# Thirteen block products of a 1x1 convolution by quarter blocks, with other products' matmuls between them

## The chip, the cores and the metric

The kernel runs on one core of a Trainium2 chip. The metric is the device time of one execution in microseconds; before the change it is 2220.28 us, the median of three runs (2220.21 to 2221.42).

## What is computed

The reference is a residual block on 8 images of 512 channels and 32x32 pixels, all in fp32:

```python
t = cbs(gn(x), cv1_w, cv1_bn, 0)             # 1x1 conv 512 -> 512, batch norm, silu
ys = [t[:, :C], t[:, C:]]                    # C = 256
for i in range(N):                           # N = 2
    yi = ys[-1]
    z = cbs(yi, m_cv1_w[i], m_cv1_bn[i], 1)  # 3x3 conv 256 -> 256
    z = bot_attention(z, m_qkv_w[i], m_rw[i], m_rh[i])   # 4 heads, 1024 positions
    z = silu(bn_eval(conv2d(z, m_cv2_w[i], 0), m_cv2_bn[i]))
    ys.append(yi + z)
return x + cbs(concatenate(ys), cv2_w, cv2_bn, 0)        # 1x1 conv 1024 -> 512
```

The change concerns the last convolution, cv2, alone.

## The kernel before

The eight images are worked off in four passes of two images, ia and ib. TensorE (PE) does nearly all the work: cv1, the 3x3 convolutions in a Winograd form (matmuls c_ps<-v_in,u, with the weights u loaded from DRAM), the attention, m2, and cv2. A tile framework puts the instructions of each engine in an order at build time; each engine then works its queue off in order.

cv2 multiplies a weight matrix of 512 x 1024 by the 1024 channels of an image with 1024 pixels. Both are cut into 2 x 2 blocks (256 outputs by 512 channels; 512 channels by 512 pixels), and the product is done in the way of Strassen and Winograd with seven block products instead of eight. The left factors are the weight blocks "11", "12", "22" and their sums s1 to s4, which are made once and kept in DRAM (load_ws); the right factors are blocks of the concatenation, "top" (y0, y1) and "bottom" (y2, y3), and their sums t1 to t4. The products are M1 = 11 x top0, M2 = 12 x bottom0, M3 = s4 x bottom1, M5 = s1 x t1, M6 = s2 x t2, M7 = s3 x t3, M4 = 22 x t4. A block product (function product) is 8 matmuls: 4 chunks of 128 channels for each of two groups of 128 outputs, over 512 pixels.

In passes 0 to 2 strassen() does this for each image. M2 is accumulated in PSUM onto M1 (tile c_1, ps1), M3 onto M5 (c_5, ps5); part3 then does M6, M7, M4 one after the other, each in a new PSUM tile c_new, and VectorE (DVE) adds each to the kept m1 in one addition of 128x1024. Each finished block of 256 outputs by 512 pixels goes through finish(i): ScalarE (ACT) writes two tiles c_out (tag "t", four buffers, in turn), GpSimd's (POOL's) queue adds x to each by an accumulating DMA and stores them. For image ib the second conv stage of the next pass follows on PE right behind cv2, with its weights u in the same ring of ten SBUF tiles as the weight blocks. In that conv each of the steps takes two of three PSUM tiles of the pool ps_big; ACT copies one part out (c_m), DVE makes c_t and the rest.

In the last pass no work follows: rest_apart() has the products of both images apart, and m4_pieces() does the last product M4 of image ib in three pieces, of 512, 256 and 256 columns. finish_last() silus the pieces, DVE adds x from tiles x_res, and SP's queue stores them.

Of the kernel before, what the change touches and what calls it, by code (L numbers as in the profile page):

```python
# [61 lines left out]
def kernel(  # L62
# [237 lines left out]

    fed = {}

    def loader(key):
        kind = key[0]
        if kind == "u":
            _, n, oc, i, cp = key
            w = ring([P, NM, 2, 2, P], "u")
            nc.sync.dma_start(w, u_dram[n][oc][i][cp])
        elif kind == "sq":
            _, n, _, j = key  # L310
            at, size = SQ[j]
            w = ring([P, size, 3, P], "sq")
            nc.sync.dma_start(w, sq_dram[n][:, at : at + size])
        elif kind == "sw":
            at, size = SQ[key[2]]
            w = ring([P, size, NX // 2, C], "sw")
            nc.sync.dma_start(w, sw_dram[:, at : at + size])
        elif kind == "w1":
            w = ring([P, NX // 2, 2 * C], "w1")
            nc.sync.dma_start(w, cv1_w.rearrange("(k p) o -> p k o", p=P)[:, ts(key[2], NX // 2)])  # L320
        elif kind == "qkv":
            w = ring([P, 3 * C], "w_qkv")
            nc.sync.dma_start(w, m_qkv_w[key[1], ts(key[3], P), :])
        elif kind == "w2":
# [172 lines left out]
    def stages(act, small, ps_big, ps_av, n_pt):  # L497
# [45 lines left out]
        def tiles_steps(yp, put, is_=(0, 1, 2), ec=None, room=None, ec_at=("rs", 4)):  # L543
# [17 lines left out]
            for i in is_:  # L561
# [13 lines left out]
                nc.gpsimd.memset(e[:, :, 0:1], 0.0)  # L575
                cleared[0] = nc.gpsimd.memset(e[:, :, F + 1 : F + 2], 0.0)
# [767 lines left out]
        def strassen(b, ws, top, tags, tile_of):  # L1344
# [46 lines left out]
            def part3(bottom, after=None):  # L1391
                t1 = kept["t1"]
                t2, t3 = sums_tile("k"), tile_of("t3").rearrange("p a c (h w) -> p a c h w", w=F)
                with tc.issue_after(after.ins) if after else nullcontext():
                    for part in range(2):
                        tt(t2[:, part], bottom[1][part], t1[:, part], ALU.subtract)
                    for part in range(2):
                        tt(t3[:, part], bottom[1][part], top[1][part], ALU.subtract)
                t4 = sums_tile("q")
# [3 lines left out]
                w12, s4 = ws("12"), ws("s4")  # L1403
                for part in range(2):
                    product(ps1, w12, bottom[0], [part], onto=True)
                    product(ps5, s4, bottom[1], [part], onto=True)
# [16 lines left out]

            return part1, part1_more, part2, part3

        def sums_apart(top, bottom, t2, t3, t4):

            for part in range(2):
                tt(t3[part], bottom[1][part], top[1][part], ALU.subtract)
            for part in range(2):  # L1430
                last = tt(t2[part], t3[part], top[0][part], ALU.add)
            yield last
            for part in range(2):
                last = tt(t4[part], t2[part], bottom[0][part], ALU.subtract)
            yield last
# [29 lines left out]
        def rest_apart(ws, kept, bottom, t2, t3, t4, new, finish):  # L1465

            m1, m5 = kept["m1"], kept["m5"]
            pss, c12 = {}, []
# [23 lines left out]
            def m6():  # L1492
                tt(m1, raw("s2", t2), m1, ALU.add)
                tt(c12[0], c12[0], m1, ALU.add)
                finish(1, c12[0])

            def m7():
                tt(m1, raw("s3", t3), m1, ALU.add)
# [3 lines left out]
            def m4():  # L1502
                tt(m1, m1, raw("22", t4), ALU.subtract)
                finish(3, m1)

            def m4_pieces(out_of):
# [16 lines left out]
                m2_half=m2_half, m2_m3=m2_m3, add_m2=add_m2, add_m3=add_m3, m6=m6, m7=m7, m4=m4, m4_pieces=m4_pieces  # L1523
# [500 lines left out]
    for p in range(NP):  # L2024
# [365 lines left out]
        if p == 0:  # L2390
            ws = {name: load_ws(name) for name in ("21", "22", "11", "12")}
# [3 lines left out]
        else:  # L2395
            feed([("ws", p, name) for name in (WS_NAMES if more else ("12", "s4", "s2", "s3", "22"))])
# [7 lines left out]
        if more:  # L2404
            feed(units(0)[:3])
# [3 lines left out]
        def tile_of(name):  # L2409
            if not cz:  # L2410
                cz.append(act.tile([P, 4, 2 * HALF], F32, tag="z", name="cz"))
            if name == "t3":
                return cz[0][:, 0:2].rearrange("p a (c f) -> p a c f", c=NM)
            return cz[0][:, 3].rearrange("p (a f) -> p a f", a=2)

        bottom_a = [[side(Y2[0], half), img2(y3a[half])] for half in range(NH)]
        if not more:
# [14 lines left out]
            whole = [ring([P, HW], "x_res") for _ in range(NO)]  # L2432
            for oc in range(NO):
                nc.sync.dma_start(whole[oc], x[ib, ts(oc, P), :])
            ts_a = [], [], []
            rest_a = s.rest_apart(w_of, heads[ia].kept, bottom_a, *ts_a, acc_tile, s.finish_apart(ia))
# [7 lines left out]
            with tc.issue_after(end.evicted.ins):  # L2444
                last = next(sums_a)
            with tc.issue_after(last.ins):
                end.spread()
            with tc.issue_after(s.inverted[0].ins):
                rest_a.add_m2()
                last = next(sums_a)  # L2450
            with tc.issue_after(last.ins):
                scaled = end.scale()
            with tc.issue_after(scaled.ins):
                rest_a.add_m3()
            last = s.m2(1, z[:, :, 1], Y2[1], lambda oc, half: img(y3b[:, half, oc, :]))
            bottom = [[side(Y2[1], half), img2(y3b[:, half])] for half in range(NH)]
            top = load_tops(ib, Y1[1], "pt", 6)
            rest_a.m6()
# [7 lines left out]
            rest_b = s.rest_apart(w_of, heads[ib].kept, bottom, *ts_b, lambda: kept_sums.pop(0), finish)  # L2466
            rest_a.m7()
            rest_a.m4()
            for t, new in zip(ts_b, (wide("k"), pt_pair(), wide("q"))):
                t.extend(new)  # L2470
            for _ in s.sums_apart(top, bottom, *ts_b):
                pass
            rest_b.m2_half()
            rest_b.m2_m3()
            rest_b.add_m2()
            rest_b.add_m3()
            rest_b.m6()
            rest_b.m7()
# [22 lines left out]
        b1, b1_more, b2, b3 = s.strassen(ib, w_of, top, {"m1": ("p3", 1), "m5": ("p4", 1)}, tile_of)  # L2501
        b1()
        b1_more()
        b2()
        vs = v_units()
# [10 lines left out]
        for g in range(G):  # L2516
            s.tiles_in(Y1[g], putter(vs, g), [2], ecs[g])
# [109 lines left out]
```

## Time and profile before

| | |
|---|---|
| median of three runs | 2220.28 us |
| the profiled execution | 2222.78 us, of which the span of the profile 2221.2 us |
| PE busy | 2192.8 us, 99% of the span |
| DVE busy | 1752.2 us, 79% |
| ACT busy | 1093.9 us, 49% |
| POOL busy | 222.0 us, 10% |
| cv2 of image ib in pass 0, M5 to M4 | 593.20 to 634.50 us |
| last product, M4 of image ib in the last pass | starts at 2205.79 us |

Rows of a timeline give the start in us, the duration, the engine, the line of the kernel, the operation, output <- inputs, shape and how many instructions the row holds; in square brackets stands how long the engine had been idle before it, and what ended that. PEld is the loading of weights into PE, which runs beside its matmuls. A row with x16 spans sixteen instructions, from the start of the first to the end of the last. An fp32 matmul leaves two records. Rows of DMA issues give the time at which POOL or SP issued the transfer, not when it ended.

### The profile page before, as it was taken

The page shows a single profiled execution, that of the slowest core. Times are in us where ns is not written, and L with a number is a line of the kernel's source. Part 1 is how long each engine was busy: PE and PEld are TensorE (multiplying, and loading weights), DVE is VectorE, ACT ScalarE, POOL GpSimd, SP SyncE. Part 2 cuts the span into 40 slices and gives each one's busy share as a digit, 9 for nine tenths or more (in the row PEclk, how much of TensorE's full clock was granted, in tenths as well). Part 3 has the DMA queues.
Part 4 walks back from the last instruction along what each step waited for, and adds up shares of the span by engine and source line. Part 5 has one row for each costly group of instructions (what it writes and reads, how often), then busy time and mean ns, then how long its engine had stood idle before and what let it go on. Part 6 is the DMA issues. An engine that isn't in the chain of part 4 may idle for free.

```text
span 2221.2 us, 40357 instructions
## 1 busy us (share of the span) xinstructions
PE 2192.8 (99%) x16330; PEld 1079.8 (49%) x16330; DVE 1752.2 (79%) x2794; ACT 1093.9 (49%) x1320; POOL 222.0 (10%) x416
## 2 busy tenths in 40 slices
PE   7999999999999999999999999999999999999998
PEld 3653437343474444734447443654344734383433
DVE  8988879878769688977857868987785877897664
ACT  7454553554225666465323676455622465336543
POOL 4322210000220000000021000000002100000001
PEclk9999999999999999999999999999999999999999
DMA  8954447312582324512268141542126701261123
GB/s 265 317 170 136 168 149 260 105 64 68 142 264 68 119 82 132 199 59 68 63 162 267 31 166 36 190 131 77 58 67 171 268 30 44 91 208 34 58 59 96
DMA packets 133799, 285.61 MB, mean 129 GB/s; under 512 B 33541, under 2 KB 61185, under 8 KB 132581
## 3 DMA queue, kind: packets, MB, share of 16 engines
q1 hardware_dynamic: 101700, 197.34, 26.9%
q0 software_dynamic: 31904, 85.61, 13.2%
q8 instruction: 131, 2.15, 0.4%
q14 instruction: 64, 0.52, 0.1%
HBM read 214.86 MB, written 68.03 MB: 127 GB/s over the span
## 4 chain that ended last, share of the span: by engine, by line
PE 90%; DVE 6%; issue 1%; DMA 1%; ACT 1%; POOL 0%; DVEq 0%; ACTq 0%; POOLq 0%
PE av_ps L1101 19%; PE l_ps L1064 18%; PE c_ps L659 10%; PE c L1338 9%; PE c_new L1338 8%; PE p_ps L940 7%; PE m_ps L1318 5%; PE x_ps L1579 4%; PE ps L529 4%; PE p_ps L946 3%; PE s_ps L1119 1%; DMA taps<-in_m_cv_w_dram 1%; DVE acc L1085 1%; PE p_ps L904 1%; PE pv_ps L946 0%
## 5 line engine op out<-in xcount | busy, mean ns | idle before, releaser
L1068 ACT ACTIVATE pt<-l_ps 128x1024 f32<-128x1024 f32 x512 | 495.7, 1023 | 328.1 <-PE l_ps L1064 252.2
L1064 PE MATMUL l_ps<-q,kr 64*64 64x512 f32 x4096 | 485.5, 590 | 0.9 <-ACT pt L1068 0.9
L1101 PE MATMUL av_ps<-pt,vT 64*64 64x512 f32 x4096 | 484.7, 590 | 1.3 <-DVE z L1109 1.1
L1085 DVE TENSOR_TENSOR acc<-acc,pt 128x1024 f32<-128x1024 f32 x362 | 442.8, 1223 | 37.6 <-ACT pt L1068 11.2
L1101 PEld LDWEIGHTS av_ps<-pt,vT 64*64 64x64 f32 x4096 | 156.0, 133 | 280.7 <-issue 233.9
L1064 PEld LDWEIGHTS l_ps<-q,kr 64*64 64x64 f32 x4096 | 157.5, 133 | 270.3 <-issue 246.3
L659 PEld LDWEIGHTS c_ps<-v_in,u 128*64 128x64 f32 x4320 | 235.8, 137 | 6.3 <-issue 6.0
L659 PE MATMUL c_ps<-v_in,u 128*64 128x128 f32 x4320 | 238.5, 273 | 0.0
L1109 DVE TENSOR_TENSOR z<-av_ps,z 128x512 f32<-128x512 f32 x64 | 44.0, 688 | 98.4 <-ACT z L1108 98.3
L1318 PE MATMUL m_ps<-z,m_sb 128*128 128x512 f32 x256 | 113.9, 593 | 0.0
L664 ACT COPY c_m<-c_ps 128x512 f32<-128x512 f32 x48 | 28.1, 586 | 159.6 <-PE c_ps L659 145.9
L940 PE MATMUL p_ps<-t_z,sq 128*128 128x512 f32 x224 | 105.9, 595 | 0.0
L501 ACT ACTIVATE t<-m_ps,bh,sh 128x512 f32<-128x512 f32 x64 | 46.3, 774 | 94.0 <-PE m_ps L1318 92.8
L1082 DVE TENSOR_TENSOR acc<-pt 128x1024 f32<-128x1024 f32 x64 | 78.1, 1221 | 13.8 <-PE s_ps L1119 8.3
L940 PE MATMUL p_ps<-z,sq 128*128 128x512 f32 x168 | 81.3, 604 | 0.8 <-ACT z L501 0.7
L1318 PEld LDWEIGHTS m_ps<-z,m_sb 128*128 128x128 f32 x256 | 47.7, 190 | 56.7 <-issue 51.4
L1177 DVE TENSOR_TENSOR z<-z,rs 128x512 f32<-128x512 f32 x64 | 42.5, 687 | 26.9 <-DMA rs<-r_dram 26.7
L501 ACT ACTIVATE z<-z,bh,sh 128x512 f32<-128x512 f32 x64 | 48.7, 809 | 25.4 <-DVE z L721 25.2
L940 PEld LDWEIGHTS p_ps<-t_z,sq 128*128 128x128 f32 x224 | 39.5, 191 | 36.5 <-issue 34.4
L501 ACT ACTIVATE c_out<-m_kept,bh,sh 128x512 f32<-128x512 f32 (+1 forms) x33 | 38.9, 1276 | 34.6 <-issue 16.2
L1579 PE MATMUL x_ps<-t_x,sw 128*128 128x512 f32 x128 | 55.9, 592 | 0.0
L1338 PE MATMUL c_new<-t_in,wss 128*128 128x512 f32 x128 | 55.9, 592 | 0.0
(343 smaller groups left out, 3169.6 us busy)
## 6 DMA issues: line engine op xcount, KB each, us to landing
u<-u SPq DMA_DIRECT2D x135, 512.0 KB
y_in<-y SPq DMA_DIRECT2D x32, 512.0 KB
rs<-r_dram SPq DMA_DIRECT2D x126, 128.0 KB
sq<-sq SPq DMA_DIRECT2D x42, 384.0 KB
x<-in_x_dram SPq DMA_DIRECT2D x28, 512.0 KB
r_in<-r SPq DMA_DIRECT2D x28, 512.0 KB
c_out<-in_x_dram POOLq DMA_DIRECT2D x56, 256.0 KB, 5.5
out_dram<-c_out POOLq DMA_DIRECT2D x56, 256.0 KB, 3.3
```

The costliest lines, as they stand in the source:

```text
L501: silued[0] = nc.scalar.activation(dst, src, AF.Silu, scale=sh[:, k : k + 1], bias=bh[:, k : k + 1])
L529: last_product[0] = nc.tensor.matmul(ps[:, half, :], w_of(k), rhs_of(k, half), start=(k == begin), stop=(k == end))
L659: conv_product[0] = nc.tensor.matmul(to[o], us[cp][:, k, row, c, o], rhs, start=(k == 0), stop=(k == NM - 1),)
L940: nc.tensor.matmul(ps[:, o, :], w[:, o, :], rhs, start=not onto, stop=True, skip_group_check=onto)
L1064: nc.tensor.matmul(ps[kh * HD : (kh + 1) * HD, hd, :], kr[r, c, o : o + HD], q[r, c, ts(half, HALF)], start=True, stop=True,)
L1068: last_exp[0] = exp = nc.scalar.activation(pt, ps, AF.Exp, scale=SCALE)
L1082: return nc.vector.tensor_tensor(accs[g], pt[0], pt[1], ALU.add)
L1085: ins = nc.vector.tensor_tensor(accs[g], accs[g], pt[i], ALU.add)
L1101: nc.tensor.matmul(avs[g][hd * HD : (hd + 1) * HD, kh, :], vT[r, j, o : o + HD], pt[i][r, hd, :], start=(j == 0), stop=(j == NJ - 1),)
L1318: nc.tensor.matmul(pss[half][:, oc, :], m2_sb[:, n, k, ts(oc, P)], ao[:, k, ts(half, HALF)], start=(k == 0), stop=(k == NM - 1),)
L1338: nc.tensor.matmul(ps[:, o, :], w[:, k, ts(o, P)], rhs[part][:, c], start=(k == 0 and not onto), stop=(k == KB - 1), skip_group_check=onto,)
L1579: nc.tensor.matmul(ps[:, o, :], w[:, c, ts(o, P)], rhs[c], start=(c == 0 and not onto), stop=(c == 1), skip_group_check=onto,)
```

## The change

Thirteen block products are done by a second level of the same scheme. Those are M6, M7 and M4 of image ib in passes 0 to 2, and in the last pass M6, M7, M4 of image ia and M6 of image ib. Weight block and right factor are cut into 2 x 2 quarters (128 outputs by 256 channels; 256 channels by 256 pixels), and seven products of quarters, each of 2 matmuls with 256 columns, take the place of the 8 matmuls with 512. The weight sums (wls2, wls3, wl22) are made once in pass 0 on DVE, stored, and loaded in the later passes; DVE makes four sums of quarters (t_q) for each right factor. by_quarters() accumulates in parts of two PSUM tiles c_q: x_ is a half of one bank into which four products are accumulated one by one, and DVE takes up its state after each; y_ and z_ share the other bank. The two tiles change places from one product to the next.

Between these short products stand the matmuls of M2 and M3 (fill_units, Beside), one by one, where before they stood ahead of M6; finish(0) comes behind the twelfth of them, finish(1) behind the last. In the last pass the eight matmuls of M7 of ib are fills too, and the sum for finish(1) is made in two additions, c12_early and c12_late. The weight tiles are loaded in another order, the three u tiles that were loaded ahead are not, two of the x_res loads go to POOL's queue, and some memsets of w_rows go from POOL to DVE.

```diff
+    L2_NAMES = ("s2", "s3", "22")
...
+    def make_l(name, w):
+        t = ring([P, 4, 2, P], f"wl{name}")
+        sums_of(blocks_of(w), [t[:, i] for i in range(4)])
+        nc.gpsimd.dma_start(l_dram[name], t)
+        return t
...
+        def quarter_sums(rhs, sums):
+            (b11, b12), (b21, b22) = quarter_blocks(rhs)
+            t1, t2, t3, t4 = sums
+            yield tt(t1, b12, b11, ALU.subtract)
+            yield tt(t2, b22, t1, ALU.subtract)
+            yield tt(t3, b22, b12, ALU.subtract)
+            yield tt(t4, b21, t2, ALU.subtract)
...
+        def by_quarters(banks, w, l, x, src, dst, op, beside):
+            Q = HALF // 2
+            x_ = banks[0][:, :Q]
+            z_, y_ = (banks[1][:, ts(j, Q)] for j in range(2))
...
+            mm(x_, a11, b11, first=True)
+            put(0, 0, x_)
+            beside()
+            mm(y_, s1, t1, first=True)
+            put(1, 1, y_)
+            beside()
+            mm(x_, s2, t2)
+            put(0, 1, x_)
+            beside()
+            mm(z_, a12, b21, last=True)
+            beside()
+            mm(x_, s3, t3)
+            put(1, 1, x_, dst)
+            beside()
+            mm(y_, s4, b22, last=True)
+            tt(dst[:, 0], dst[:, 0], banks[1], op)
+            beside()
+            mm(x_, a22, t4, last=True)
+            last = put(1, 0, x_)
+            beside()
+            banks.reverse()
+            return last
+
+        def quarter_banks():
+            return [ps_big.tile([P, HALF], F32, tag="big", name="c_q") for _ in range(2)]
...
+            def by_quarters3(quarters, bottom, ps1, ps5, m1, m5, w12, s4, t4):
+                ends, u3, c12 = [], tile_of("o2"), tile_of("o1")
+                for part in (1, 0):
+                    fill_units(ends, ps1, w12, bottom[0], [part], True)
+                    fill_units(ends, ps5, s4, bottom[1], [part], True)
...
+                ends[11] = lambda: (first(), behind_m2())
+                ends[15] = lambda: (second(), behind_m3())
+                for _ in range(3):
+                    ends.pop(0)()
+                beside = Beside(ends, (2, 3))
+                banks = quarter_banks()
+                by_quarters(banks, ws("s2"), l2.of("s2"), quarters["s2"], m1, m1, ALU.add, beside)
+                x = quarters_of(halves(t4), l2.room("22"))
+                beside.steps.append(x.steps)
+                by_quarters(banks, ws("s3"), l2.of("s3"), quarters["s3"], m1, u3, ALU.add, beside)
+                beside.rest()
+                tt(m5, m5, u3, ALU.add)
+                finish(2, m5)
+                by_quarters(banks, ws("22"), l2.of("22"), x, u3, u3, ALU.subtract, beside)
+                while ends:
+                    ends.pop(0)()
+                return lambda: finish(3, u3)
...
+            def c12_early():
+                c12.append(new())
+                tt(c12[0], m5, m1, ALU.add)
+            def c12_late():
+                tt(c12[0], pss["s4"], c12[0], ALU.add)
                 finish(1, c12[0])
...
+            def m7_whole():
+                tt(m1, pss["s3"], m1, ALU.add)
+                tt(m5, m5, m1, ALU.add)
+                finish(2, m5)
...
-            feed([("ws", p, name) for name in (WS_NAMES if more else ("12", "s4", "s2", "s3", "22"))])
+            if more:
+                feed([("ws", p, name) for name in WS_NAMES])
+                feed([("wl", p, name) for name in L2_NAMES])
+            else:
+                feed([("ws", p, name) for name in ("12", "s4")])
+                feed([(kind, p, name) for name in L2_NAMES for kind in ("ws", "wl")])
...
-        if more:
-            feed(units(0)[:3])
...
-            rest_b.m6()
-            rest_b.m7()
+            rest_a.m4(q)
+            q[1].rest()
+            rest_b.fills_m7(fills)
+            q[1].steps.append(sums_b)
+            rest_b.m6(q, False)
+            q[1].rest()
+            rest_b.c12_early()
+            while fills:
+                fills.pop(0)()
+            rest_b.c12_late()
+            rest_b.m7_whole()
             flush()
             rest_b.m4_pieces(out_of)
...
-            s.tiles_in(Y1[g], putter(vs, g), [2], ecs[g])
+            s.tiles_in(Y1[g], putter(vs, g), [2], ecs[g], clear=nc.vector)
```

On PE, cv2 of image ib in pass 0 looked like this before. c_4630 holds M1 and M2, c_4641 M5 and M3, c_new the products of s2, s3 and 22 in turn; ypad and y3b are the halves of bottom.

```order
L1338 MATMUL c_4630<-ypad_70,ws_3991 128x512 x4
L1338 MATMUL c_4641<-ypad_70,ws_s_3996 128x512 x4
L1338 MATMUL c_4630<-y3b,ws_3991 128x512 x4
L1338 MATMUL c_4641<-y3b,ws_s_3996 128x512 x4
L1338 MATMUL c_new<-t_in,ws_s_3994 128x512 x8
L1338 MATMUL c_new<-cz,ws_s_3995 128x512 x8
L1338 MATMUL c_new<-t_in,ws_3987 128x512 x8
L659 MATMUL c_ps<-v_in,u 64x128 x288
```

After the change the same place begins as follows (c_4627 and c_4638 are the tiles that were c_4630 and c_4641; ws_s_3997 is s2, wls_4649 its sums).

```order
L1386 MATMUL c_4627<-y3b,ws_3992 128x512 x3
L1402 MATMUL c_q<-t_in,ws_s_3997 128x256 x2
L1386 MATMUL c_4627<-y3b,ws_3992 128x512
L1402 MATMUL c_q<-t_q,wls_4649 128x256 x2
L1386 MATMUL c_4638<-y3b,ws_s_3999 128x512
L1402 MATMUL c_q<-t_q,wls_4649 128x256 x2
L1402 MATMUL c_q<-t_in,ws_s_3997 128x256 x2
L1386 MATMUL c_4638<-y3b,ws_s_3999 128x512
L1402 MATMUL c_q<-t_q,wls_4649 128x256 x2
L1386 MATMUL c_4638<-y3b,ws_s_3999 128x512
L1402 MATMUL c_q<-t_in,wls_4649 128x256 x2
L1402 MATMUL c_q<-t_q,ws_s_3997 128x256 x2
```

The matmuls with 128x512 that stood together, ahead of the products, now stand singly between matmuls of 128x256 of the first product; the products of s3 and 22 follow in the same manner.

On POOL the DMAs of the four finishes of image ib in pass 0 stood in this order before (c_out_4760 and 4764 belong to finish(0), 4779 and 4783 to finish(1), 4798 and 4802 to finish(2)). A line with in_x_dram adds x, a line with out_0_dram stores.

```order
L1388 DMA c_out_4760<-in_x_dram 128x512
L1388 DMA c_out_4764<-in_x_dram 128x512
L1389 DMA out_0_dram<-c_out_4760 128x512
L575 MEMSET w_rows_4866 128x32
L1389 DMA out_0_dram<-c_out_4764 128x512
L576 MEMSET w_rows_4866 128x32
L1388 DMA c_out_4779<-in_x_dram 128x512
L1388 DMA c_out_4783<-in_x_dram 128x512
L1389 DMA out_0_dram<-c_out_4779 128x512
L1389 DMA out_0_dram<-c_out_4783 128x512
L1388 DMA c_out_4798<-in_x_dram 128x512
L1388 DMA c_out_4802<-in_x_dram 128x512
```

After the change (4827 and 4831 belong to finish(0), 4840 and 4844 to finish(2), 4866 and 4870 to finish(1)):

```order
L1499 DMA c_out_4827<-in_x_dram 128x512
L1499 DMA c_out_4831<-in_x_dram 128x512
L1500 DMA out_0_dram<-c_out_4827 128x512
L1499 DMA c_out_4840<-in_x_dram 128x512
L1500 DMA out_0_dram<-c_out_4831 128x512
L1499 DMA c_out_4844<-in_x_dram 128x512
L591 MEMSET w_rows_6567 128x32
L592 MEMSET w_rows_6567 128x32
L1500 DMA out_0_dram<-c_out_4840 128x512
L1500 DMA out_0_dram<-c_out_4844 128x512
L1499 DMA c_out_4866<-in_x_dram 128x512
L1499 DMA c_out_4870<-in_x_dram 128x512
```

finish(2) is now second and finish(1) third, and the first loads of finish(2) stand between the stores of finish(0).

On DVE the end of the last pass was this before: the addition for M6 and c12 (L1493, L1494), for M7 (L1498, L1499), and for the pieces of M4 (L1519), with the additions of x_res.

```order
L1493 TENSOR_TENSOR m_kept<-c_new,m_kept 128x1024
L1494 TENSOR_TENSOR cz<-cz,m_kept 128x1024
L1556 TENSOR_TENSOR cz<-cz,x_res 128x512 x2
L1498 TENSOR_TENSOR m_kept<-c_new,m_kept 128x1024
L1499 TENSOR_TENSOR m_kept<-m_kept 128x1024
L1556 TENSOR_TENSOR c_out<-c_out,x_res 128x512
L1519 TENSOR_TENSOR m_kept<-m_kept,c_new 128x512
L1556 TENSOR_TENSOR c_out<-c_out,x_res 128x512
L1519 TENSOR_TENSOR m_kept<-m_kept,c_new 128x256
```

After the change (L1408 and L1425 are additions of by_quarters, L1666 is c12_early, L1669 c12_late, L1684 and L1685 are M7's):

```order
L1408 TENSOR_TENSOR m_kept<-m_kept,c_q 128x256 x3
L1425 TENSOR_TENSOR m_kept<-m_kept,c_q 128x512
L1408 TENSOR_TENSOR m_kept<-m_kept,c_q 128x256
L1666 TENSOR_TENSOR cz<-m_kept 128x1024
L1669 TENSOR_TENSOR cz<-c_new,cz 128x1024
L1684 TENSOR_TENSOR m_kept<-c_new,m_kept 128x1024
L1743 TENSOR_TENSOR cz<-cz,x_res 128x512
L1685 TENSOR_TENSOR m_kept<-m_kept 128x1024
L1743 TENSOR_TENSOR cz<-cz,x_res 128x512
L1705 TENSOR_TENSOR m_kept<-m_kept,c_new 128x512
```

Two additions of 128x1024 stand between the last one of M6 and those of M7.

More of the change, by code (lines that the diff above doesn't have):

```diff
@@ L2402, in w_of, with l_of, room_of @@
                 return got[name]
-        if more:
-            feed(units(0)[:3])
+        l_made = {}
+        def l_of(name):
+            if name not in l_made:
+                l_made[name] = take(("wl", p, name))
+            return l_made[name]
+        def room_of(*tiles):
+            return [t[:, j] for t in tiles for j in range(2)]
         top = load_tops(ia, None if more else Y1[0])
```

191 lines of the change are left out of this document (154 added, 37 removed).

## The prediction

> **What bounds the kernel now.** I read the page's shares first, then the chain that ended last, then the timelines of PE, DVE, ACT and POOL around the places that the change touches, and last the tail.
>
> ```profile
> span 2221.2 us, 40357 instructions
> PE 2192.8 (99%) x16330; PEld 1079.8 (49%) x16330; DVE 1752.2 (79%) x2794; ACT 1093.9 (49%) x1320; POOL 222.0 (10%) x416
> PE 90%; DVE 6%; issue 1%; DMA 1%; ACT 1%; POOL 0%; DVEq 0%; ACTq 0%; POOLq 0%
> ```
>
> PE is busy 99% of the span and is 90% of the chain. So a microsecond taken out of PE's queue is a microsecond of the kernel, as long as what replaces it keeps PE fed, and a wait put into that queue costs its full length. The profiled execution took 2222.78 us, 2.5 us (0.11%) above the median 2220.28; I work out differences on its rows and take them from the median. About 0.2% (4.4 us) is what a measurement can tell from no change.
>
> **What a product costs by each way.**
>
> ```profile
> 593.20 7.03 PE L1338 MATMUL c<-t_in,ws_s 128*128 128x512 f32 x16
> 600.07 3.60 PE L1338 MATMUL c<-ypad,ws 128*128 128x512 f32 x8
> ...
> 2209.23 3.21 PEld L1514 LDWEIGHTS c_new<-t_in,ws 128*128 128x128 f32 x15 [0.24 <-issue]
> 1755.42 1.05 PE L946 MATMUL p_ps<-sq,z 128*128 128x128 f32 x8
> 1756.31 1.06 PE L946 MATMUL p_ps<-sq,t_z 128*128 128x128 f32 x8
> ```
>
> An fp32 matmul leaves two records. A product of 8 matmuls is 16 records, 600.07 - 593.20 = 6.87 us, so 0.429 us a record of 512 columns. For 256 columns the last pieces of M4 give the pace: 15 loads in 3.21 us are 14 steps and one load of 0.19, so 0.2157 us a record. A product by quarters is 14 matmuls, 28 records: 28 x 0.2157 = 6.04 us. It saves 0.83 us; 13 products save 10.8 us of PE. The filling matmuls are the same as before, only moved, and cost PE nothing.
>
> Does each record's weight load spoil this? It is 0.19 us, and the row of 128 columns shows records 0.89 us / 8 = 0.111 apart (1755.42 to 1756.31), so loads hide under even shorter matmuls. The Trainium skill, "TensorE: Matmul & The Clock Gate", section Back-to-back issue gap, speaks against the change: in a stream of load and matmul pairs the spacing falls much slower than the columns, from about 131 ns at 512 to about 81 ns at 128. Read in a straight line, 256 columns would take some 98 ns, three quarters of 512 columns and not half, and 28 of them more than 16 of the long ones (an estimate: 2.7 against 2.1 us a product, 8 us slower over 13). The trace disagrees: 0.2157 is half of 0.429. The sum goes by the trace.
>
> **Passes 0 to 2, image b: 9 products, -7.4 us of PE.** Three products in each pass, 3 x 0.83 = 2.5 us, so the conv behind them starts 2.5 us earlier if DVE and the weights keep up.
>
> DVE gets four quarter sums of 128x512 (0.69 each), five additions of 128x256 (0.42) and one of 128x512 for a product, in place of one of 128x1024 (1.22): 5.6 - 1.2 = 4.3 us at most, 13 us more in a stage in which it idles this much:
>
> ```profile
> 600.27 1.23 DVE L1401 TENSOR_TENSOR t_in<-t_in,ypad 128x1024 f32<-128x1024 f32 x1 [6.30 <-PE c L1338]
> 614.00 0.69 DVE L606 SCALAR_TENSOR_TENSOR v_in<-w_d 128x512 f32<-128x512 f32 x1 [11.37 <-PE c L1338]
> ```
>
> The eight sums of s2 and s3 (5 us) fall into the first gap, 6.30 us, the additions of the first product into the second. Inside a product PE takes up a PSUM part that DVE must first have read after two other matmuls of 256 columns or of filling, 1.7 to 2.6 us, against 0.2 + 0.42 us for the answer; only in pass 0 is the first addition close (about 0.7 us of room behind the sums). I charge nothing, upper bound 1 us a pass. The nine more loads of 512 KB on SP and the three stores on POOL I charge at nothing, for the DMA engines are far from full in the stretches that hold them. The u loads of the conv are no longer begun early; they wait for free places of the ring:
>
> ```profile
> 593.40 0.32 SPq L308 DMA_DIRECT2D u<-u  x1
> 593.77 1.14 SPq L111 DMA_DIRECT2D x<-in_x_dram  x2
> 600.26 27.79 SPq L308 DMA_DIRECT2D u<-u  x5
> ```
>
> Six were issued here in the products' time, beside the three early ones, and the conv takes three in 5.24 us. Now each tile of cv2 weights that is done with (11, s1, ls2, s2, 12, ls3, s3, s4) makes room for one, eight before the conv and two at its start, so I charge nothing. Cover gone: one u load late, some 2 us a pass.
>
> **The outputs of image b: a wait that the change makes.** A finish is two silus into two c_out tiles, a DMA that adds x to each, and a store. Four c_out tiles serve, so a finish waits for the stores of the last but one. Before, the order was 0, 1, 2, 3; now it is 0, 2, 1, 3: finish(3) waits for the stores of finish(2), not of finish(1). And finish(3) stands on ACT ahead of conv's second copy c_m. These are the rows, of pass 0 and (the last three) of pass 2:
>
> ```profile
> 610.62 2.29 ACT L501 ACTIVATE c_out<-c,bh,sh 128x512 f32<-128x512 f32 x2 [9.34 <-PE c L1338]
> 643.50 0.59 ACT L664 COPY c_m<-c_ps 128x512 f32<-128x512 f32 x1 [2.32 <-PE c_ps L659]
> 648.78 0.59 ACT L664 COPY c_m<-c_ps 128x512 f32<-128x512 f32 x1 [4.70 <-PE c_ps L659]
> 634.50 31.66 PE L659 MATMUL c_ps<-v_in,u 128*64 128x128 f32 x576
> 612.18 1.90 POOL L1388 DMA_DIRECT2D c_out<-in_x_dram  x2 [6.12 <-ACT c_out L501]
> 616.94 0.58 POOL L1389 DMA_DIRECT2D out_dram<-c_out  x1 [2.87 <-DMA c_out<-in_x_dram]
> 620.34 0.57 POOL L1389 DMA_DIRECT2D out_dram<-c_out  x1 [2.65 <-DMA c_out<-in_x_dram]
> 629.73 0.86 POOL L1388 DMA_DIRECT2D c_out<-in_x_dram  x1 [0.19 <-issue]
> 635.33 0.57 POOL L1389 DMA_DIRECT2D out_dram<-c_out  x1 [0.72 <-DMA c_out<-in_x_dram]
> 635.88 1.82 POOL L1388 DMA_DIRECT2D c_out<-in_x_dram  x2
> 646.01 0.57 POOL L1389 DMA_DIRECT2D out_dram<-c_out  x1 [2.72 <-DMA c_out<-in_x_dram]
> 1722.24 0.56 POOL L1389 DMA_DIRECT2D out_dram<-c_out  x1 [0.70 <-DMA c_out<-in_x_dram]
> 1724.86 1.33 ACT L501 ACTIVATE c_out<-m_kept,bh,sh 128x512 f32<-128x512 f32 x1 [0.22 <-DMA out_dram<-c_out]
> 1727.56 1.33 ACT L501 ACTIVATE c_out<-m_kept,bh,sh 128x512 f32<-128x512 f32 x1 [1.37 <-DMA out_dram<-c_out]
> ```
>
> Let E be the start of the conv. From now on: the twelfth fill releases finish(0), and behind it stand one quarter product, one fill and the third product with its three fills, 0.86 + 0.86 + 6.04 + 2.58 = 10.3 us: finish(0) starts at E - 10.3. Its second store was issued 9.7 us after its start (610.62 to 620.34), so now at E - 0.6. POOL issues in order, and finish(2)'s second load stands right behind that store: E + 0. Its landing releases the second store of finish(2): in 5.6 us as at 629.73 to 635.33, when few u loads ran, or in up to 9.6 as at 636.4 (the second of the pair at 635.88) to 646.01, when conv's u loads ran. E + 0 lies between these two (E - 4.8 and E + 1.9); I interpolate 8.5. That store holds the tile until it has landed, 5.3 us (1722.24 to 1727.56; the first of that pair some 3.9): I take 4.6. So finish(3)'s second silu starts at E + 13.1, bounds 9.5 (5.6 + 3.9) and 14.9 (9.6 + 5.3).
>
> When is that too late? The silu is 1.33, then c_m, then DVE's two c_t, which in the rows ended 1.9 us after c_m started, with the hand-overs 3.4 us in all. What waits for them is the second half of conv's third step, whose three PSUM tiles go round: PE gets there right before the third copy c_m, at 648.78 - 0.2 - 634.50, E + 14.0. So PE stands still if the silu starts after E + 10.6: by 2.5 us in a pass at my value, by nothing at the lower bound, by 4.3 us at the upper. Before, pass 2 had this wait too (1.37 us, on ACT), but at 1727.56, E + 7.3 of its conv, within the room. Three passes: +7.5 us (0 to 13).
>
> **The last pass: 4 products, -3.3 us of PE, and a longer tail.** Sums and the first additions find DVE idle again. At the end stand these:
>
> ```profile
> 2205.79 7.05 PE L1514 MATMUL c_new<-t_in,ws 128*128 128x512 f32 x24
> 2205.99 1.23 DVE L1498 TENSOR_TENSOR m_kept<-c_new,m_kept 128x1024 f32<-128x1024 f32 x1 [1.25 <-PE c_new L1338]
> 2207.25 1.22 DVE L1499 TENSOR_TENSOR m_kept<-m_kept 128x1024 f32<-128x1024 f32 x1
> 2208.51 2.39 ACT L501 ACTIVATE c_out<-m_kept,bh,sh 128x512 f32<-128x512 f32 x2 [4.49 <-DVE m_kept L1499]
> 2211.17 1.93 ACT L501 ACTIVATE c_out<-m_kept,bh,sh 128x512 f32<-128x512 f32 x2 [0.27 <-DVE m_kept L1519]
> 2213.93 0.84 ACT L501 ACTIVATE c_out<-m_kept,bh,sh 128x256 f32<-128x256 f32 x1 [0.82 <-DVE m_kept L1519]
> 2214.79 0.42 DVE L1556 TENSOR_TENSOR c_out<-c_out,x_res 128x256 f32<-128x256 f32 x1 [0.85 <-ACT c_out L501]
> ```
>
> Let T be the start of M4's pieces (2205.79), now 3.3 us earlier. Before, m5's silus began at T + 2.7 and the last addition ended at T + 9.4. Now the last quarter product ends two fills (1.7 us) ahead of T; its addition, then c12_early and c12_late (1.25 each, one behind the other) end at T + 1.4, then the two additions behind m7 at T + 3.9, with an x_res addition between them T + 4.6. From there ACT has 2.39 + 1.93 + 0.84 us without a pause, and the last addition ends at about T + 10.6: 1.2 us later against T. Kept: about 2 of 3.3 us (bounds 0.9, if the x_res additions get in the way more, and 3.3).
>
> **Sum.** -7.4 + 7.5 - 2.0 = -1.9 us: 2220.3 - 1.9 = 2218.4.
>
> **Rivals.** (1) The stores are quick enough, and nothing waits. For it: loads of finish(2) start some 2 us earlier against E than before, and the DMA engines are at 76% around E, as the row below shows. Then -7.4 - 2 = -9.4, 2210.9, with no loss in the tail 2209.6. (2) Slower: the same queue at its upper bound or beyond. For it: in E + 1.5 to E + 17 the engines are full.
>
> ```profile
> 628.00:636.00 8.00, 8.00 (x44) 4.13 (x44) 3.41 (x3) 3.79 (x4) 3.00 (x5) 1.00 0.76 164
> 636.00:644.00 8.00, 8.00 (x152) 8.00 (x149) 4.52 (x9) 3.42 (x4) 2.51 (x5) 1.00 0.95 259
> 644.00:652.00 8.00, 8.00 (x150) 8.00 (x148) 7.12 (x14) 0.67 (x2) 2.38 (x3) 1.00 1.03 391
> ```
>
> (The two last columns are the DMA share and GB/s.) A store that takes 7 us in this, behind a load of 9.6, ends at E + 16.6: 6 us of waiting a pass, 18 - 9.4 = +8.6, 2229. It decides from a landing later than E + 15.2, where 3 x 4.6 us eat 9.4 and 4.4 more are the smallest slowdown that can be told. (3) The change doesn't shorten PE: a record of 256 columns among other matmuls takes over 6.87 / 28 = 0.245 us, the load no longer hidden. At 0.32, three quarters of 0.429, a product takes 9.0 us: +28 us, 2248. Against it: 0.2157 in the row above. By the skill's rule this is the case. (4) DVE answers late in the quarters, 1 us a pass and 1 in the last: +4, beside the store wait 2222.
>
> **How the numbers follow.** My forecast with a wait of 1.5 to 4.6 us a pass, (4) included: 0.45, 2215.9 to 2224.7. Rival (1), with waits up to 1.5 us: 0.36. Rival (2): 0.16. Rival (3): 0.03. So faster 0.36, same 0.45, slower 0.19. The range leaves out rival (3), most of (2) and the fastest part of (1): 2210.5 to 2225.5.
>
> **What would show it.** Records of c_q 0.216 us apart; conv of image b 2.5 us earlier against the pass's attention in passes 0 to 2; then ACT's finish(3) with idle time put down to the store of c_out, its second silu at about E + 13, and PE idle 2 to 3 us before c_ps in the third step, put down to DVE's c_t. If that idle time is missing, rival (1) is right and I have put the stores too late. In the tail, m5's silus 4 to 5 us behind M4's start.

## The result, and the profile after

The changed kernel takes 2240.2 us (median of 4 runs, 2239.17 to 2241.7), the kernel before 2220.24 us: a ratio of 1.009, 95% interval 1.0072 to 1.0107. I had forecast 2218.4 in a range of 2210.5 to 2225.5. The change made the kernel 20 us slower. One of the five executions of early0 below took 5964.18 us at a granted clock of 0.415, and its figures there leave that one out.

The head of the page after, to be read against the one before:

```profile
span 2237.9 us, 40845 instructions
PE 2190.8 (98%) x16486; PEld 1115.3 (50%) x16486; DVE 1801.7 (81%) x2935; ACT 1094.8 (49%) x1320; POOL 223.1 (10%) x409
PE 72%; DVE 12%; issue 8%; DMA 5%; POOL 1%; ACT 1%; SPq 0%; POOLq 0%; DVEq 0%; ACTq 0%
```

PE's share of the chain has fallen from 90% to 72%, and DVE, "issue" and DMA, 8% together before, are now 25%. PE's busy time fell by only 2 us, not by the 10.8 that the products save: somewhere matmuls became slower. The starts of the conv stages in PE's timeline tell where (us; conv a is the one ahead of cv2 of the images, conv b the one behind cv2 of ib):

| | before | after | difference |
|---|---|---|---|
| start of the first conv | 106.6 | 104.4 | -2.2 |
| conv a to conv b, passes 0, 1, 2 | 294.6, 295.3, 295.2 | 292.1, 292.7, 292.7 | -7.6 |
| conv b to the next conv a, passes 0, 1, 2 | 247.7, 247.7, 225.5 | 257.4, 256.9, 234.9 | +28.4 |
| last conv a to the start of M4 | 260.1 | 256.9 | -3.1 |
| start of M4 to the end | 15.4 | 16.6 | +1.2 |

The sum is +16.7 us, the difference of the spans (the profiled executions, 2222.78 and 2239.34 us, lie closer together than the medians). (The first line belongs to the start of the kernel, ahead of any change; it lay between 104.0 and 106.6 in the profiles of this study.) The products won what was forecast. Everything was lost in three stages, conv b, 9 us and more in each. This is PE's timeline there, pass 0:

```profile
629.89 8.96 PE L675 MATMUL c_ps<-v_in,u 128*64 128x128 f32 x160
643.23 7.98 PE L675 MATMUL c_ps<-v_in,u 128*64 128x128 f32 x96 [4.38 <-issue]
651.46 7.21 PE L675 MATMUL c_ps<-v_in,u 128*64 128x128 f32 x128 [0.25 <-issue]
```

The conv begins at E = 629.89, 2.5 us earlier against conv a than before. Then PE stands still for 4.38 us, in the second of the steps, and the next 96 records take 7.98 us, 0.083 us each, where the first 160 took 0.056. The table by stretches has the reason for the second part in its column of the granted clock (third from the right, ahead of DMA share and GB/s); first in steps of 8 us, then finer around the pause:

```profile
628.00:636.00 8.00, 8.00 (x121) 7.44 (x121) 2.15 (x3) 0.00 (x0) 3.13 (x6) 1.00 1.00 283
636.00:644.00 8.00, 3.62 (x62) 3.41 (x58) 2.16 (x5) 3.02 (x3) 1.45 (x3) 0.85 1.05 352
644.00:652.00 8.00, 7.75 (x102) 7.53 (x100) 4.29 (x10) 3.63 (x4) 3.16 (x5) 0.72 1.02 303
652.00:660.00 8.00, 7.79 (x143) 7.54 (x140) 7.97 (x17) 0.58 (x1) 1.31 (x2) 1.00 1.01 278
```

```profile
640.00:641.00 1.00, 0.00 (x0) 0.00 (x0) 0.00 (x0) 0.91 (x1) 0.00 (x0) 1.00 1.10 365
641.00:642.00 1.00, 0.00 (x0) 0.00 (x0) 0.16 (x1) 0.81 (x2) 0.00 (x0) 0.80 1.02 356
643.00:647.00 4.00, 3.77 (x36) 3.80 (x38) 3.36 (x8) 1.32 (x1) 2.38 (x3) 0.50 1.02 390
648.00:649.00 1.00, 1.00 (x18) 1.00 (x17) 0.00 (x0) 0.69 (x1) 0.00 (x0) 0.79 1.21 205
649.00:650.00 1.00, 1.00 (x24) 1.00 (x20) 0.00 (x0) 1.00 (x2) 0.35 (x1) 1.00 0.93 272
```

From 644 to 652 PE is busy for 7.75 of 8 us and gets through 102 records instead of some 150. The 0.85 and 0.72 are averages: the clock fell to 0.50 at 641.6, inside the pause, and came back to 1.00 at 648.4, 5.2 us after PE had gone on. Half of these 6.8 us, 3.4 us, is lost. So the stage costs 9.2 us more, of which 5.6 us are idle time and nearly all the rest is the slow clock.

Why the pause? ACT's timeline, and POOL's with its DMAs:

```profile
619.71 2.33 ACT L517 ACTIVATE c_out<-c,bh,sh 128x512 f32<-128x512 f32 x2 [20.56 <-PE c L1386]
622.45 2.37 ACT L517 ACTIVATE c_out<-m_kept,bh,sh 128x512 f32<-128x512 f32 x2 [0.41 <-DVE m_kept L1568]
636.40 1.30 ACT L517 ACTIVATE c_out<-cz,bh,sh 128x512 f32<-128x512 f32 x1 [11.58 <-DMA out_dram<-c_out]
640.09 1.29 ACT L517 ACTIVATE c_out<-cz,bh,sh 128x512 f32<-128x512 f32 x1 [2.38 <-DMA out_dram<-c_out]
641.18 0.62 ACT L680 COPY c_m<-c_ps 128x512 f32<-128x512 f32 x1
648.31 1.30 ACT L517 ACTIVATE c_out<-cz,bh,sh 128x512 f32<-128x512 f32 x1 [1.85 <-DMA out_dram<-c_out]
649.41 0.62 ACT L680 COPY c_m<-c_ps 128x512 f32<-128x512 f32 x1
```

```profile
621.31 1.90 POOL L1499 DMA_DIRECT2D c_out<-in_x_dram  x2 [18.94 <-ACT c_out L517]
629.68 0.58 POOL L1500 DMA_DIRECT2D out_dram<-c_out  x1 [6.48 <-DMA c_out<-in_x_dram]
630.99 0.71 POOL L1500 DMA_DIRECT2D out_dram<-c_out  x1
631.56 1.02 POOL L1499 DMA_DIRECT2D c_out<-in_x_dram  x1
643.13 0.57 POOL L1500 DMA_DIRECT2D out_dram<-c_out  x1 [3.68 <-DMA c_out<-in_x_dram]
```

The rows of ACT are finish(0), finish(2), the two silus of finish(1), the first c_m, the last silu of finish(3) and the second c_m. Of the 11.58 us that ACT is idle ahead of finish(1), the first 4.7 go by until DVE has made its sum; from about E + 0 on it waits 6.9 us, and again 2.38 us, for the stores of finish(0) to free its c_out tiles. The first c_m stands behind it in ACT's queue and comes at E + 11.3; before, it came 3.8 us after the conv's start. DVE and then PE wait for it, as DVE's rows show: PE goes on at 643.23, right behind the second c_t (the profile itself calls PE's wait "issue").

```profile
641.84 0.69 DVE L701 TENSOR_TENSOR c_t<-c_ps,c_m 128x512 f32<-128x512 f32 x1 [11.41 <-ACT c_m L680]
642.45 0.68 DVE L702 TENSOR_TENSOR c_t<-c_ps,c_m 128x512 f32<-128x512 f32 x1
```

The second c_m is late in the same way, behind finish(3), but PE's pause has already given it time. The addition DMAs of finish(0) took 8.4 us from issue to the store behind them, its second store 9.1 us (630.99 to 640.09).

### The profile page after: what moved, and what is told of

It is laid out like the page before. It is cut to its first block, busy times and chain, and to the rows that moved or that the text cites. A ratio compares the mean times of both kernels' runs of the same rounds, so it can differ in the third digit from the quotient of the medians.

```text
span 2237.9 us, 40845 instructions
## 1 busy us (share of the span) xinstructions
PE 2190.8 (98%) x16486; PEld 1115.3 (50%) x16486; DVE 1801.7 (81%) x2935; ACT 1094.8 (49%) x1320; POOL 223.1 (10%) x409
## 4 chain that ended last, share of the span: by engine, by line
PE 72%; DVE 12%; issue 8%; DMA 5%; POOL 1%; ACT 1%; SPq 0%; POOLq 0%; DVEq 0%; ACTq 0%
PE av_ps L1117 19%; PE l_ps L1080 18%; PE c_ps L675 6%; PE p_ps L956 6%; PE ps L545 4%; PE x_ps L1766 4%; PE m_ps L1334 4%; PE p_ps L962 3%; DMA c_out<-in_x_dram 3%; PE c L1354 2%; PE s_ps L1135 1%; DMA out_dram<-c_out 1%; PE c_q L1402 1%; PE c_new L1386 1%; DVE acc L1101 1%
## 5 line engine op out<-in xcount | busy, mean ns | idle before, releaser
L675 PE MATMUL c_ps<-v_in,u 128*64 128x128 f32 x4320 | 248.4, 278 | 17.2 <-issue 15.5
L675 PEld LDWEIGHTS c_ps<-v_in,u 128*64 128x64 f32 x4320 | 242.6, 140 | 25.2 <-issue 22.3
L701 DVE TENSOR_TENSOR c_t<-c_ps,c_m 128x512 f32<-128x512 f32 (+1 forms) x64 | 35.2, 550 | 46.3 <-ACT c_m L680 46.3
L517 ACT ACTIVATE c_out<-cz,bh,sh 128x512 f32<-128x512 f32 x18 | 22.9, 1310 | 98.4 <-DMA out_dram<-c_out 51.5
```

Of the source, the lines that this page charges most:

```text
L517: silued[0] = nc.scalar.activation(dst, src, AF.Silu, scale=sh[:, k : k + 1], bias=bh[:, k : k + 1])
L675: conv_product[0] = nc.tensor.matmul(to[o], us[cp][:, k, row, c, o], rhs, start=(k == 0), stop=(k == NM - 1),)
```

## The experiments

What the kernels of one call ran against is the kernel before on the same chip; its median there was 2220.77, 2220.37 and 2221.04 us.

**Tiles of their own.** finish(1) and finish(3) write elsewhere, so ACT waits for no store:

```diff
+                own = {1: "p1", 3: "p2"}.get(i) if l2 else None
+                pair = act.tile([P, 2, HALF], F32, tag=own, name="c_out", bufs=1) if own else None
                 for at in range(2):
-                    t = act.tile([P, HALF], F32, tag="t", name="c_out", bufs=4)
+                    t = pair[:, at] if own else act.tile([P, HALF], F32, tag="t", name="c_out", bufs=4)
```

> The changed kernel, but finish(1) and finish(3) of image ib in passes 0 to 2 write into tiles of their own (p1 and p2, free by then), so no finish waits for another's stores. Theory 1 (the wait of finish(1) and finish(3) for c_out tiles holds up c_m, and that PE): the second conv stage behind cv2 of ib takes 31.4 us again instead of 40.1 to 40.6, PE has no idle time over 1 us in it, the granted clock stays at 1.00, and the time falls by the 28 us that these stages lost, to 2211 to 2213. Theory 2 (the DMA engines are overfull around the start of the conv, so that u loads or x additions come late whatever tiles they use): the conv stays at 38 us or more, the time above 2232.

Measured: 2239.24 us, ratio 1.0079 (1.0062 to 1.0096). Half of theory 1 came true: conv b takes 31.66 us in each pass, as before the change, with no idle time. And the time hardly fell. (Theory 2 had the time right, but not the conv, which it put at 38 us or more.) The waits of PE and its timeline in pass 0:

```profile
PE p_ps L956 <- POOL t_z L934: 21.3, 3, 8.3
```

```profile
631.28 31.66 PE L675 MATMUL c_ps<-v_in,u 128*64 128x128 f32 x576
662.87 1.98 PE L956 MATMUL p_ps<-z,sq 128*128 128x512 f32 x4
673.18 3.78 PE L956 MATMUL p_ps<-t_z,sq 128*128 128x512 f32 x4 [8.33 <-POOL t_z L934]
```

PE waits three times, 21.3 us in all, for t_z, a subtraction that stands on POOL behind the DMAs of the four finishes:

```profile
655.87 0.58 POOL L1502 DMA_DIRECT2D out_dram<-c_out  x1 [6.93 <-DMA c_out<-in_x_dram]
659.07 1.82 POOL L1501 DMA_DIRECT2D c_out<-in_x_dram  x2
668.31 0.58 POOL L1502 DMA_DIRECT2D out_dram<-c_out  x1 [7.42 <-DMA c_out<-in_x_dram]
671.27 0.57 POOL L1502 DMA_DIRECT2D out_dram<-c_out  x1 [2.38 <-DVE z L737]
671.85 1.27 POOL L934 TENSOR_TENSOR t_z<-z 128x512 f32<-128x512 f32 x1
```

A store waits on POOL until its addition has landed, and all that is behind it waits too. (For the last store the profile names DVE's z; the store reads only its own tile, so its addition is the likelier cause. What t_z itself reads was ready by 656.1, when ACT's silus of z had ended.) The granted clock halved here as well, for 6.8 us at each wait. In the kernel before, the same chain began at 612.18, 22 us ahead of the conv; in the changed kernel at 621.31, 8.6 us ahead of it. So, as the next runs bear out, the tiles were one way in which this late chain reached PE, not its cause. Theory 1 fell, and a third one took its place: the chain of DMAs is too late, and it reaches PE by the tiles or, if not, by the queue.

**The last pass alone.** Passes 0 to 2 with whole products again:

```diff
-            ib, w_of, top, {"m1": ("p3", 1), "m5": ("p4", 1)}, tile_of, SimpleNamespace(of=l_of, room=room_b)
+            ib, w_of, top, {"m1": ("p3", 1), "m5": ("p4", 1)}, tile_of
```

> The changed kernel with cv2 of ib in passes 0 to 2 as before (whole products, old order of finishes; the sums of weights are still made and loaded): only the last pass is by quarters. Theory 1 (the loss is all in passes 0 to 2): last pass 3.1 us shorter up to M4, tail 1.2 us longer, so about 2 us under the kernel before, 2218; if the 2.1 us that the first pass gained ahead of its first cv2 belong to the change, 2216. Rival (the last pass or the additional loads cost as well): 2221 or more.

Measured: 2219.48 us, ratio 0.9994 (0.9985 to 1.0004): the loss is gone, and the gain, 1.3 us by the medians where I had expected about 2, can't be told from none. By its profile the last conv a to M4 took 256.9 us, 3.1 us less than before, and the last addition came 1.1 us later behind M4's start (the end of the span 1.9 us). The twelve sums of weights and the additional loads, which this kernel keeps, cost nothing that shows.

**What a pause of PE costs.** The kernel before, with repeated copies of c_m in front of the one that DVE needs:

```diff
+                    for _ in range(15 if after else 0):
+                        nc.scalar.copy(m24, slots(inner_ps, 1))
                     copied = nc.scalar.copy(m24, slots(inner_ps, 1))
```

> The kernel before, with 15 needless repetitions of the first copy c_m of the conv behind cv2 of ib, on ACT, some 0.5 us each, in passes 0 to 2: the copy that DVE waits for is some 7.5 us late, of which 3 to 4 us are room, so PE stands still for about 4 us in each of the three stages. If an idle microsecond of PE costs a microsecond, the conv takes about 35.7 instead of 31.4 us and the kernel 13 us more. If the granted clock falls after it, as to 0.72 to 0.85 in the changed kernel, the conv takes 38 to 39.5 us and the kernel 20 to 24 us more.

> As idle15 with 9 repetitions: the copy 4.5 us late, PE idle for about 1 us in each of the three stages. If idle time costs itself only, the conv takes 32.4 us and the kernel 3 us more. If a short idle time also brings the clock down, the conv takes 34 us or more and the kernel 8 us more; if only a longer one does, the granted clock stays at 1.00 here.

Measured: 2238.91 us with 15 copies and 2230.76 us with 9 (one run each), 18.1 and 10.0 us more. With 15, PE was idle in conv b for 3.5, 3.9 and 4.5 us (each time 3.47 us in one piece, then up to 0.99) and each stage became 5.8 to 6.1 us longer; 0.5 to 1.3 us of that are neither these pauses nor, as told below, the clock. With 9 copies the pause was 2.53 us in each pass, where I had expected about 1. Here are pass 0 and pass 1 of that kernel, timeline and stretches:

```profile
643.44 24.59 PE L659 MATMUL c_ps<-v_in,u 128*64 128x128 f32 x416 [2.53 <-DVE c_t L688]
1190.64 22.93 PE L659 MATMUL c_ps<-v_in,u 128*64 128x128 f32 x416 [2.53 <-DVE c_t L688]
```

```profile
640.00:648.00 8.00, 5.47 (x71) 5.26 (x69) 6.11 (x13) 4.46 (x7) 2.96 (x4) 0.79 1.05 368
1188.00:1196.00 8.00, 5.47 (x102) 5.39 (x100) 6.90 (x15) 3.73 (x5) 2.97 (x4) 1.00 1.04 356
```

The same pause, and behind it the same 416 records took 24.59 us once and 22.93 the other time, 1.66 us apart: in pass 0 the granted clock was 0.50 for 3.4 us (0.79 is the average of the stretch), in pass 1 it stayed at 1.00. It stayed there in pass 2 of both kernels too, in idle15 behind a pause of 3.47 us that had brought it down in passes 0 and 1. Between my two expectations the truth lay in the middle for idle15, and for idle9 it depended on the pass.

The length of a pause doesn't decide alone, then; its place does. In each trace all changes of the granted clock lie whole multiples of 3.413 us apart. Cut the time into such windows: in conv b of the changed kernel, of idle15 and of idle9 a full clock fell at the end of each window in which PE had been idle for 2.2 us or more, and of none with 1.96 us or less, and it came back at the end of the first window with no pause over 0.4 us. (Near 72 us, ahead of these stages, 1.93 us were enough in one profile, so the border lies close to there.) The 2.53 us of idle9 lay in one window in pass 0 and across two in passes 1 and 2 (1.7 and 2.0 us in the larger part); so did the 3.47 us in pass 2 of idle15 (1.9 us).

The Trainium skill, "TensorE: Matmul & The Clock Gate", section What's actually happening, describes such a gate: after an idle window of about 3.4 us the clock is halved, and it returns after a busy one; the windows run freely, so it matters where in them a pause falls. The half clock, the 3.413 us and the return agree. The same page's section HAM oscillation asks for no gaps over 3.4 us; here 2.53 us were enough in one pass and 3.47 us not in another, and the measurement decides.

**Theory 3: t_z away from POOL's queue.** On top of own tiles:

```diff
-                                t = first_sum(summed, nc.gpsimd)
+                                t = first_sum(summed, nc.vector)
```

> own_tiles (finish(1) and finish(3) with tiles of their own), and the one subtraction t_z behind the conv of ib, which stands on POOL behind the four finishes' DMAs, is made on DVE instead. Theory 3 (the finishes' DMAs, each store behind its addition in POOL's queue, are a chain of 12 us a finish that starts 12 us later than before; whoever stands behind it waits: ACT's c_m through the tiles, or POOL's t_z through the queue): no wait is left, PE goes from the conv into p_ps without a pause, 2.5 us a pass and 2 in the last are won: 2210 to 2213. Rival (the chain reaches someone else behind it on POOL, or DVE, 99% busy at the end of the conv, pays for t_z): 2216 or more.

Measured: 2210.28 us, ratio 0.9951 (0.9934 to 0.9968). No wait is left: conv b takes 31.66 us, with p_ps right behind it. This is the gain that the products bring when nobody stands behind the chain.

**The chain earlier.** Only the order of the fills is changed, all of M2 first:

```diff
                 for part in (1, 0):
                     fill_units(ends, ps1, w12, bottom[0], [part], True)
+                for part in (1, 0):
                     fill_units(ends, ps5, s4, bottom[1], [part], True)
...
-                first, second = ends[11], ends[15]
-                ends[11] = lambda: (first(), behind_m2())
+                first, second = ends[7], ends[15]
+                ends[7] = lambda: (first(), behind_m2())
```

> The changed kernel with another order of the fills alone: the eight of M2 first, then the eight of M3, so finish(0) of ib starts behind the eighth fill, some 9 us earlier. Tiles and queues as in the changed kernel. Theory 3: the chain of DMAs starts 9 us earlier; finish(1) finds its tiles free near the start of the conv, the first c_m isn't held up, finish(3)'s tiles are free at 10 to 13 us behind it: PE idle at most 2 us a pass, conv 31.4 to 34 us instead of 40.4, time 2212 to 2219. Rival (DMA engines too full whatever the order, each finish late by the same): conv over 37 us, time over 2230.

> Both: M2's fills first, and tiles of their own for finish(1) and finish(3); t_z stays on POOL. Theory 3: ACT never waits, conv 31.4 us; the last addition and t_z on POOL come 9 us earlier than in own_tiles, where t_z made PE wait 8.3 us, so at most 1 us of waiting is left there: 2210 to 2214. Rival (t_z's place in the queue alone decides, not when the chain starts): PE waits over 5 us for t_z, 2228 or more.

Measured: early0 2212.17 us (median of four), ratio 0.9959 (0.9943 to 0.9975); early0_own 2211.3 us, 0.9956 (0.994 to 0.9973). In both conv b takes 31.66 us without a pause. ACT and POOL in early0, pass 0, where the conv starts at 632.1:

```profile
613.28 2.33 ACT L517 ACTIVATE c_out<-c,bh,sh 128x512 f32<-128x512 f32 x2 [11.95 <-PE c L1386]
631.89 2.40 ACT L517 ACTIVATE c_out<-cz,bh,sh 128x512 f32<-128x512 f32 x2 [4.77 <-issue]
635.84 0.58 ACT L680 COPY c_m<-c_ps 128x512 f32<-128x512 f32 x1 [1.55 <-PE c_ps L675]
639.90 2.71 ACT L517 ACTIVATE c_out<-cz,bh,sh 128x512 f32<-128x512 f32 x2 [3.48 <-DMA out_dram<-c_out]
642.41 0.62 ACT L680 COPY c_m<-c_ps 128x512 f32<-128x512 f32 x1
```

```profile
634.65 1.82 POOL L1499 DMA_DIRECT2D c_out<-in_x_dram  x2
647.21 1.82 POOL L1499 DMA_DIRECT2D c_out<-in_x_dram  x2
658.88 0.57 POOL L1500 DMA_DIRECT2D out_dram<-c_out  x1 [2.49 <-DMA c_out<-in_x_dram]
659.47 1.29 POOL L934 TENSOR_TENSOR t_z<-z 128x512 f32<-128x512 f32 x1
```

finish(0) starts 18.8 us ahead of the conv instead of 10.2, finish(1) finds its tiles free, and t_z runs at 659.47, 4 us ahead of the conv's end. finish(3) still waits 3.48 us for the stores of finish(2), and this costs nothing, since the second c_m has room. The same tiles and the same queues as in the changed kernel, with the DMA engines as full (a share of 0.86 to 1.04 from 612 to 652), and 28 us faster by one order: with a chain of this length, it is when it starts that decides.

**Which leg is too long.** The changed kernel without the DMAs that add x in these finishes:

```diff
-                    nc.gpsimd.dma_start(t, rows_of(x, i, at), accum_op=ALU.add)
+                    if not l2:
+                        nc.gpsimd.dma_start(t, rows_of(x, i, at), accum_op=ALU.add)
```

> The changed kernel without the DMAs that add x in the finishes of ib in passes 0 to 2 (x is missing from these blocks of the output); tiles, order and stores as in the changed kernel. It tells which leg of a finish was too long. Theory 3 (store behind addition in one queue): the stores of finish(0) are issued 8 us earlier, right behind its silus, finish(1) finds its tiles at the start of the conv, no wait of more than 1 us is left on PE, 2210 to 2213. Rival (the stores alone, 6 to 9 us each under the u loads, already hold the tiles too long): conv at 35 us or more, over 2222.

Measured: 2212.0 us, ratio 0.9955 (0.994 to 0.997), conv b 31.66 us without a pause. Stores alone don't hold the tiles too long; addition and store one behind the other do. (Without the additions the DMA engines also have less to move; the run doesn't part the two.)

**The tail, and all together.** On top of own_dve, own_dve_tail makes M3 + m5 as soon as M3 is there, one addition instead of two behind the last quarter product:

```diff
+            rest_b.add_m3()
-            rest_b.m6(q, False)
+            rest_b.m6(q)
             q[1].rest()
-            rest_b.c12_early()
             while fills:
                 fills.pop(0)()
-            rest_b.c12_late()
```

> As own_dve, and in the last pass the sum for finish(1) of ib is made as before the change: M3 + m5 as soon as M3 is there, one addition behind M6, instead of c12_early and c12_late behind the last quarter product. Theory (these two additions make the tail longer): m5's silus start 1.2 us earlier against M4's start, and the kernel is about 1.2 us faster than own_dve. Rival (the tail is set by ACT and the x_res additions): the same time as own_dve within 0.3 us.

> The version put together: M2's fills first, tiles of their own for finish(1) and finish(3), t_z on DVE, the sum for finish(1) of the last pass in one addition behind M6. Each of these alone or in pairs left no wait in the conv, so there is nothing more to win there: 2209 to 2211, as own_dve_tail; if the time is under 2208, the finishes' DMAs cost something in own_dve that its profile doesn't show as a wait.

Measured: own_dve_tail 2210.28 us (0.995, 0.9934 to 0.9967), the same median as own_dve. In its profile m5's silus start 3.4 us behind M4's start instead of 4.7, yet the last addition ends only 0.65 us earlier, since ACT then waits for the pieces of M4; 0.65 us is too little to tell here, and the 1.2 us that I expected weren't there. all_four took 2209.38 us, ratio 0.9946 (0.9932 to 0.9959), 11.7 us less than before: the fastest kernel of the study, though not by more than its interval.

## Why the prediction was wrong

- *A product by quarters saves 0.83 us, 7.4 us in passes 0 to 2.* Right: 7.6 us. The page of lines gives 379 ns for a record of c_q as for the last pieces of M4, and products 0.86 us for four records. Rival (3), the exposed weight load, is out.
- *DVE keeps up, u loads and weights cost nothing.* Right: in the products no pause is over 0.15 us, with DVE busy 7.96 of 8 us in one stretch. Rival (4) is out.
- *The last pass wins 3.3 us and its tail loses 1.2.* Right: 3.1 and 1.1 to 1.2; m5's silus at M4 + 4.7 (forecast 4.6), the last addition at M4 + 10.5 (10.6).
- *The outputs of ib.* This is the step that failed: "PE stands still if the silu starts after E + 10.6: by 2.5 us in a pass at my value". The mechanism was named, and it is what happened, but three things in it were wrong. First, I followed only finish(3) and the second c_m. finish(1) waits in the same way for finish(0)'s tiles, and it stands ahead of the first c_m, which has less room: its second silu started at E + 10.2, and PE paused for 4.4 to 4.8 us one step earlier. Second, the flights were sized too small. I took 9.7 us from the start of finish(0) to its second store, 8.5 for finish(2)'s load, 4.6 for the store behind it. After the change it was 11.3 (619.71 to 630.99), 11.6 (631.56 to 643.13) and 5.2 (643.13 to 648.31), so finish(3)'s second silu came at E + 18.4 instead of E + 13.1; finish(0)'s second store, which I hadn't followed, took 9.1. The rows of before were taken with the DMA engines partly idle; after the change they were at 0.90 to 1.05 from 620 on. That three u loads and an x load, issued 0.4 to 2.5 us ahead of finish(0)'s DMAs, made them so slow fits the rows (before the change one u load stood there; in early0 three did, and the second store came after 10.7 us) but wasn't tried by itself. Third, I priced a pause of PE at its length. It cost 9.2 us for 5.6 us of pauses, since the clock was halved for 6.8 us. In the sum the term of 7.5 us (0 to 13) measured 28.4.
- *Rival (1), no wait: 2210.9.* This is what the products are worth, 2210.28 in own_dve. It was right about the gain and wrong about the chain. *Rival (2)*, 2229 with a chance of 0.16, had the right sign, and even its bound was too small.
- The view that would have told me was one I had: POOL's rows of before show the chain of the four finishes end with t_z, right behind the last store and only 8 us before PE needs it (at 667.91).

```profile
655.20 0.58 POOL L1389 DMA_DIRECT2D out_dram<-c_out  x1 [6.82 <-DMA c_out<-in_x_dram]
657.98 0.57 POOL L1389 DMA_DIRECT2D out_dram<-c_out  x1 [2.20 <-DVE c_r L710]
658.56 1.29 POOL L918 TENSOR_TENSOR t_z<-z 128x512 f32<-128x512 f32 x1
667.91 1.88 PE L940 MATMUL p_ps<-t_z,sq 128*128 128x512 f32 x4
```

A chain of 46 us (612.18 to 658.56) that starts 13.7 us later against the conv has nowhere to go.

## What to carry to other kernels

When a change moves work that ends in a chain of transfers, follow the chain to its last consumer, in each queue that it passes, before pricing what the moved work saves; here 10 us of products stood against 28 us behind the outputs. Removing the first wait that a profile names isn't removing the cause: with free tiles the same lateness came back at POOL's t_z, almost microsecond for microsecond, and what got rid of it was an earlier start, a shorter chain, or free tiles together with a queue without others' work. Price a pause of TensorE at its length and, where the granted clock falls, half of the time at half clock on top, here 1.7 or 3.4 us.

## What the runs showed of the hardware that I had not expected

The granted clock in these traces is 1.00 or 0.50, and it changes only at whole multiples of 3.413 us. In the conv stages a full clock fell at the end of each such window with 2.2 us or more of idle PE and of none with 1.96 us or less, so the same pause of 2.53 us was followed by a half clock, 1.66 us, in one pass and by none in another. A DMA that adds 256 KB to a tile took about 5 to 7 us from issue to the store behind it where the DMA engines' share was 0.76 to 0.82 over 8 us, and 6 to 12 us where it was 0.90 to 1.05.
